# Layer 0, q and k: one 1x1 product per block of pixels for all 192 channels, into one z tile

## The chip, the cores and the metric

The kernel runs on one core of a Trainium2 chip. The metric is the device time of one execution in microseconds (us), as the median of several runs. Times inside an execution come from the hardware profile of one run. Its engines are PE (TensorE's matmuls), PEld (TensorE's weight loads, which overlap the matmuls), DVE (VectorE), ACT (ScalarE), POOL (GpSimd) and SP (SyncE, which here only issues transfers).

## What is computed

The input is an fp32 image batch of shape (4, 48, 256, 256). Four layers follow each other, and each adds to its input a function of the group-normalised input. The change lies in layer 0, which is, cut to what matters:

```python
hidden = conv1x1(gn(x), w_hidden) + b_hidden            # 48 -> 288 channels
qkv = depthwise3x3(hidden, w_dw) + b_dw                 # zero padding
q, k, v = split(qkv, 3)                                 # 96 channels each
out = irfft2(rfft2(q_patch) * rfft2(k_patch))           # on 8x8 patches
normed = (out - mean_c(out)) / sqrt(var_c(out) + eps)   # over the 96 channels
x = x + conv1x1(v * (normed * gamma + beta), w_out) + b_out
```

Layers 1 and 2 are gated layers with an 8x8 Fourier mask and a depthwise convolution; layer 3 gates 8x8 blocks by pooled values.

## The kernel before

Layer 0 works in two passes over the pixels. Each has N = 64 steps (4 images, 16 strips of 16 rows). The first pass makes q and k (192 channels), correlates their patches and keeps the normalised result in DRAM; the second makes v (96 channels), multiplies and projects. Both use the class `Strips`, once with `thirds` = 2 (name qk), once with `thirds` = 1 (name v). In the profile the tiles of the first carry `_qk`, those of the second `_v`.

A strip's 1x1 product, the method `mixed`, takes the pixels as the stationary operand. `xn` holds the strip as blocks of 6 rows by 18 columns, so that each block is 108 pixels with their borders. There are two halves of rows (u), sixteen blocks across (j) and two halves of the partitions (h, at partitions 0 and 64), 64 blocks in all. The stationary operand is one block, 49 input rows (48 channels and a row for the bias) by 108 pixels. The moving operand is the scaled weight matrix `w1`, restricted to 96 channels. The result, 108 pixels by 96 channels, goes into a PSUM tile `h_ps`, which holds four blocks j for both h, 768 values a partition. A copy on ACT or DVE, by turns, moves it to `z`, in the layout channel by block. There is one `z` tile for each third of 96 channels, `z0` and `z1`, each with a single buffer. For q and k a step is 128 products and 16 copies.

The method `depthwise` then multiplies, for each channel, the table `d` (109 pixels by 64 outputs) with that channel's 64 blocks of `z` (`c_ps`, L386). The pixels of `z` are rows 0 to 107; row 108 holds ones for the bias.

The loop of the first pass issues in step n: `mixed(n)`; `arrange(n+1)` on POOL, which fills `xn` from the loaded strip `x`; `load(n+2)`; `stats_ahead(n)`, which reads rows of the next image by transfers from ACT's queue into two `xstat` tiles and takes their statistics on DVE (L411); `attend(n-2)`; the transfers `fetch(n-1)` on SP; `convolve(n)`, the depthwise part with its copies `s` on ACT (L441) and their transfers on SP. `attend` is a chain: transform of q and k (`f_ps`, L478), copy of q on ACT (L490), product with k on DVE (L495), inverse transform (`o_ps`, L505), copy on ACT (L509); then the mean (`mu`, L520) on DVE, its subtraction on POOL (L522), the square on ACT (`sq`, L527), the variance on DVE (`var`, L529 and L530), the power and the scaling on POOL (L531, L532), the store (L533). The scaling of one half (`scale`) runs inside `convolve`.

All PSUM tiles of the pass share one pool of four buffers (`ps2`, 128 x 2 x 512). Each engine executes its own instructions in order. That order is made by a planner that starts from the order of the program, and puts an instruction where its own estimate of times lets it start; a few instructions in `attend`, marked `here`, keep the order of the program. The gated layers have an order of their own, pinned by hand.

Of the kernel before, what the change touches and what calls it, by code (L numbers as in the profile page):

```python
# [10 lines left out]
F32 = mybir.dt.float32  # L11
# [6 lines left out]
C = 48  # L18
# [155 lines left out]
def conv_stack_kernel(ctx: ExitStack, tc: tile.TileContext, t: dict):  # L174
    nc = tc.nc
# [44 lines left out]
    def evacuate(dst, src):  # L220
        turn[0] += 1
        if turn[0] % 2:
            nc.scalar.copy(dst, src)
        else:
            nc.vector.tensor_copy(dst, src)


    def layer0():
# [5 lines left out]
        NJ, PX, K = 16, 108, 109  # L234
# [17 lines left out]
        class Strips:  # L252


            def __init__(self, name, c_first, thirds, order, wp, sb, psum, spare, nx):
                self.name, self.c_first, self.thirds = name, c_first, thirds
                self.wp, self.sb, self.psum = wp, sb, psum
                nch = 96 * thirds
                self.d = d = wp.tile([K, nch, 64], F32, tag="d", name=f"d_{name}")
                for o in range(0, 64, 8):  # L260
                    basis = sb.tile([10, 8, K], F32, tag=spare[0], name=f"basis_{name}_{o}", bufs=spare[1])
                    nc.scalar.dma_start(basis, t["ones"][:, order, o : o + 8, :])
                    for i in range(0, 8, 2):
                        ps = self.ps2(f"d_ps_{name}_{o}_{i}")
                        for k in range(2):
                            nc.tensor.matmul(
                                ps[:K, k, :nch], basis[:, i + k, :],
                                taps[:, c_first : c_first + nch], start=True, stop=True,
                            )
                        evacuate(  # L270
                            d[:, :, o + i : o + i + 2],
                            ps[:K, :, :nch].rearrange("p n c -> p c n"),
                        )

                self.zs = [
                    wp.tile([K, 96, 64], F32, tag=f"z{m}", name=f"z_{name}_{m}") for m in range(thirds)
                ]
                for z in self.zs:
                    nc.gpsimd.memset(z[96:K], 1.0)


                self.xts = [
                    wp.tile([HC + 1, 10, W], F32, tag=f"x{i}", name=f"x_{name}_{i}") for i in range(nx)
                ]
                self.beside = [set() for _ in range(nx)]
                for xt in self.xts:
                    nc.gpsimd.memset(xt, 1.0)
                self.xn = wp.tile([HC + 1, 2, NJ, 6, 18], F32, tag="xn", name=f"xn_{name}")
                nc.gpsimd.memset(self.xn, 0.0)
# [63 lines left out]
            def mixed(self, n):  # L353
                b, s = steps[n]
                if s == 0:
                    self.weights_of(b)
                k = 0
                for m, z in enumerate(self.zs):
                    c0 = self.c_first + 96 * m
                    to = z[0:PX].rearrange("p c (h u j) -> p h c u j", h=2, u=2)  # L360
                    for u in range(2):
                        for j0 in range(0, NJ, 4):
                            ps = self.ps2(f"h_ps_{self.name}_{n}_{m}_{u}_{j0}")
                            for j in range(4):
                                for h in range(2):
                                    at = slice(64 * h, 64 * h + C + 1)
                                    nc.tensor.matmul(  # L367
                                        ps[0:PX, h, 96 * j : 96 * j + 96],
                                        self.xn[at, u, j0 + j].rearrange("p r c -> p (r c)"),
                                        self.w1[at, c0 : c0 + 96], start=True, stop=True,  # L370
                                    )
                            k += 1
                            copy = nc.scalar.copy if k % 2 else nc.vector.tensor_copy
                            copy(  # L374
                                to[:, :, :, u, j0 : j0 + 4],
                                ps[0:PX, :, 0:384].rearrange("p h (j c) -> p h c j", j=4),
                            )

            def depthwise(self, n, m, put):

                for q in range(3):
                    ps = self.ps2(f"c_ps_{self.name}_{n}_{m}_{q}")
                    for k in range(16):
                        for e in range(2):
                            c = 48 * e + 16 * q + k
                            nc.tensor.matmul(  # L386
                                ps[64 * e : 64 * e + 64, k // 8, 64 * (k % 8) : 64 * (k % 8) + 64],
                                self.d[:, 96 * m + c, :], self.zs[m][:, c, :], start=True, stop=True,
                            )
                    put(q, ps)  # L390


        with ExitStack() as st:
            wp = st.enter_context(tc.tile_pool(name="l0aw", bufs=1))
# [184 lines left out]
        with ExitStack() as st:  # L579
            wp = st.enter_context(tc.tile_pool(name="l0bw", bufs=1))  # L580
# [7 lines left out]
            for h in range(2):  # L588
                at, ch = slice(64 * h, 64 * h + C), slice(C * h, C * h + C)
# [113 lines left out]
            for b in range(B):  # L703
                ps = v.ps2(f"gn1_ps_{b}")
# [643 lines left out]
```

## Time and profile before

| what | value |
|---|---|
| time, median of 3 runs | 13026.5 us (13022.06 to 13051.78) |
| the profiled execution's own time | 13011.09 us |
| its span | 13009.1 us |
| mean granted TensorE clock | 0.945 |
| PE busy | 11869.5 us (91%) |
| PEld busy | 9389.8 us (72%) |
| DVE busy | 8029.6 us (62%) |
| ACT busy | 5848.6 us (45%) |
| POOL busy | 3678.6 us (28%) |
| first and last product of h for q and k | 152.4 and 3055.2 us |
| first and last product of h for v | 3207.0 and 5002.7 us |

The busy shares are means over four layers with different limits, so the first pass of layer 0 has to be read by itself, from 152 us to about 3085 us. A row of a group gives line, engine, operation, output and inputs, then for a matmul the stationary operand as rows times columns and the moving operand as rows by columns, then the number of instructions, their busy time and the mean time of one. After the second bar stands the idle time of the engine just before them and what ended it. Busy time counts overlapping instructions once. The duration of one matmul record is longer than its distance from the next, since they are pipelined: what it costs is read from the distance.

### The profile page before, as it was taken

Reading aid. Unit: us, or ns where it says so; the run is one execution under the profiler, and the core shown is the slowest. Engines: PE = TensorE matmul, PEld = TensorE weight load, DVE = VectorE, ACT = ScalarE, POOL = GpSimd, SP = SyncE. Lnnn points to the kernel's source line nnn. Section 1 sums busy time; section 2 is a strip of 40 time slices with the busy share of each in tenths; the row PEclk is TensorE's granted clock in tenths of the full one; section 3 lists DMA queues with packets and bytes.
Section 4 is the critical chain, followed back from the end, with each engine's and each line's share of the span. In section 5 each row is a group of like instructions: output and inputs, shape, how many; then the busy total and the mean of one; then the engine's idle time right before and its main releaser. Section 6 shows DMA issues by size and latency. Waiting matters only on the chain.

```text
span 13009.1 us, 473453 instructions
## 1 busy us (share of the span) xinstructions
PE 11869.5 (91%) x217556; PEld 9389.8 (72%) x217556; DVE 8029.6 (62%) x8422; ACT 5848.6 (45%) x7294; POOL 3678.6 (28%) x4549
## 2 busy tenths in 40 slices
PE   5899999998999999999998999989999989999976
PEld 5567777776888887777776777767777767777754
DVE  4666666665444444666665666665666666666678
ACT  1345555554444443444443444434444434444456
POOL 2356565665222222112112112111121121121111
PEclk8799999998999998999998999989999989999987
DMA  6666666664444443555554554544555545555555
GB/s 147 191 203 208 205 210 207 209 210 152 119 117 121 119 123 80 111 110 107 105 111 92 105 110 104 108 93 94 106 105 108 111 88 106 109 107 108 109 134 192
DMA packets 378785, 1708.61 MB, mean 131 GB/s; under 512 B 100181, under 2 KB 100786, under 8 KB 280802
## 3 DMA queue, kind: packets, MB, share of 16 engines
q1 hardware_dynamic: 202656, 907.70, 26.3%
q0 software_dynamic: 146560, 731.59, 24.1%
q10 hardware_dynamic: 27586, 39.03, 1.1%
q8 instruction: 1715, 28.10, 0.9%
q14 instruction: 268, 2.20, 0.1%
HBM read 832.42 MB, written 584.91 MB: 109 GB/s over the span
## 4 chain that ended last, share of the span: by engine, by line
PE 59%; DMA 13%; ACT 12%; DVE 8%; issue 5%; POOL 1%; SPq 1%; ACTq 0%; DVEq 0%; POOLq 0%
PE c_ps L955 14%; DMA z<-z 8%; PE y_ps L882 8%; ACT z L926 5%; ACT z L918 5%; PE h_ps_qk L367 4%; PE v_ps L647 4%; PE f_ps L478 3%; PE c_ps_qk L386 3%; PE h_ps_v L367 3%; PE c_ps_v L386 3%; PE xo_ps L992 3%; PE z_ps L908 3%; PE o_ps L505 2%; DMA xstat<-in_x 2%
## 5 line engine op out<-in xcount | busy, mean ns | idle before, releaser
L955 PEld LDWEIGHTS c_ps<-z,d 100*64 100x64 f32 x76032 | 2490.0, 146 | 788.5 <-issue 324.0
L955 PE MATMUL c_ps<-z,d 100*64 100x64 f32 x76032 | 2601.7, 230 | 416.9 <-DMA z<-z 161.4
L961 ACT ACTIVATE g<-c_ps 128x512 f32<-128x512 f32 x1188 | 695.7, 597 | 3544.7 <-PE c_ps L955 3539.7
L962 DVE TENSOR_TENSOR g<-g,c_ps 128x512 f32<-128x512 f32 x1188 | 802.6, 685 | 1599.8 <-ACT g L961 1599.6
L886 DVE TENSOR_TENSOR yf<-y_ps,mask 128x768 f32<-128x768 f32 x1536 | 1377.6, 951 | 413.5 <-PE y_ps L882 413.5
L882 PE MATMUL y_ps<-w_in,f 49*128 49x96 f32 x24576 | 1511.5, 279 | 21.6 <-issue 19.6
L882 PEld LDWEIGHTS y_ps<-w_in,f 49*128 49x128 f32 x24576 | 1445.0, 192 | 57.8 <-issue 22.3
L933 POOL DMA_DIRECT2D z<-z x384 | 200.3, 522 | 4515.6 <-ACT z L926 4426.3
L908 PE MATMUL z_ps<-yf,dft 64*64 64x512 f32 x9216 | 1104.8, 606 | 10.9 <-issue 4.5
L926 ACT COPY z<-z_ps 64x1024 f32<-64x1024 f32 x1024 | 1073.0, 1074 | 24.4 <-PE z_ps L908 5.6
L918 ACT COPY z<-z_ps 64x512 f32<-64x512 f32 x1536 | 856.6, 610 | 284.6 <-PE z_ps L908 251.1
L367 PE MATMUL h_ps_qk<-w_qk,xn_qk 49*108 49x96 f32 x16384 | 890.4, 270 | 60.5 <-DVE z_qk L374 48.2
L367 PEld LDWEIGHTS h_ps_qk<-w_qk,xn_qk 49*108 49x108 f32 x16384 | 864.7, 185 | 81.3 <-DVE z_qk L374 60.3
L966 DVE STREAM_TRANSPOSE g<-g 128x2048 f32<-128x2048 f32 x396 | 911.3, 2301 | 5.1
L992 PE MATMUL xo_ps<-g,w_out 24*64 24x512 f32 x12288 | 842.1, 599 | 28.7 <-ACT z L926 27.4
L926 DVE COPY z<-z_ps 64x1024 f32<-64x1024 f32 x512 | 619.4, 1210 | 399.7 <-DMA z<-carry 208.6
L386 PEld LDWEIGHTS c_ps_qk<-z_qk,d_qk 109*64 109x64 f32 x24576 | 777.8, 138 | 41.5 <-issue 29.5
L386 PE MATMUL c_ps_qk<-z_qk,d_qk 109*64 109x64 f32 x24576 | 788.3, 223 | 5.6 <-issue 5.4
L478 PE MATMUL f_ps<-t,l_fft 64*94 64x384 f32 x4096 | 758.1, 509 | 34.0 <-ACT f L490 31.6
L522 POOL TENSOR_TENSOR o<-o,mu 128x1536 f32<-128x1536 f32 x128 | 443.6, 3466 | 1109.4 <-DVE mu L521 813.9
L1000 DVE TENSOR_TENSOR res<-xo_ps,res 112x1024 f32<-112x1024 f32 x512 | 614.8, 1222 | 186.4 <-PE xo_ps L992 159.1
L992 PEld LDWEIGHTS xo_ps<-g,w_out 24*64 24x64 f32 x12288 | 298.7, 131 | 557.3 <-issue 221.4
(194 smaller groups left out, 17402.2 us busy)
## 6 DMA issues: line engine op xcount, KB each, us to landing
z<-z SPq DMA_DIRECT2D x1152, 203.9 KB
t<-s SPq DMA_DIRECT2D x512, 384.0 KB
t<-t SPq DMA_DIRECT2D x256, 768.0 KB
n<-o POOLq DMA_DIRECT2D x128, 768.0 KB, 5.2
kept<-n SPq DMA_DIRECT2D x128, 768.0 KB
xf<-x POOLq DMA_DIRECT2D x256, 384.0 KB, 11.7
res<-x POOLq DMA_DIRECT2D x248, 384.0 KB, 12.6
x<-res POOLq DMA_DIRECT2D x248, 384.0 KB, 5.4
```

The costliest lines, as they stand in the source:

```text
L367: nc.tensor.matmul(ps[0:PX, h, 96 * j : 96 * j + 96], self.xn[at, u, j0 + j].rearrange("p r c -> p (r c)"), self.w1[at, c0 : c0 + 96], sta ...
L386: nc.tensor.matmul(ps[64 * e : 64 * e + 64, k // 8, 64 * (k % 8) : 64 * (k % 8) + 64], self.d[:, 96 * m + c, :], self.zs[m][:, c, :], star ...
L478: nc.tensor.matmul(ps[0:94, e, 0:384], fft[at, 0:94], patches[n, m, r][at, rp, 24 * ch : 24 * ch + 24, :].rearrange("p c u -> p (c u)"), s ...
L882: first(i + j == 0, nc.tensor.matmul(ps[:, i, 96 * j : 96 * j + 96], f[at, 4 * h + j, :], w_in[at, m, :], start=True, stop=True,))
L886: pin(nc.vector.tensor_tensor(y[:, :, :, 4 * h : 4 * h + 4], ps[:, :, 0:384].rearrange("p i (j c) -> p c i j", j=4), mask[:, m].rearrange( ...
L908: first(q == 2 and p + v == 0, nc.tensor.matmul(to[64 * v : 64 * v + 64], dft[at, 1, at], y[at, c0 : c0 + 16].rearrange("p c i j -> p (c i ...
L918: pin(nc.scalar.copy(columns(p, 48 * v + 32, 48 * v + 48), last[64 * v : 64 * v + 64, p].rearrange("p (c i j) -> p c i j", i=2, j=16),))
L926: pin(copy(columns(p, 48 * v, 48 * v + 32), ps[64 * v : 64 * v + 64].rearrange("p q (c i j) -> p (q c) i j", i=2, j=16),))
L955: first(v + k == 0, nc.tensor.matmul(ps[p0 : p0 + 64, v, f0 : f0 + nj], d[rows, HID * v + 48 * m + c, :], z[rows, us, 48 * v + c, 1 : NP + ...
L962: pin(nc.vector.tensor_tensor(to, to, of[:, 1], ALU.mult))
L966: pin(nc.vector.transpose(flat, flat))
L992: first(i + k == 0, nc.tensor.matmul(ps[h][k // 2][64 * i : 64 * i + 64, k % 2, :], w_out[at, m, :], gs[m][at, j0 : j0 + 16].rearrange("p ...
```

## The change

`mixed` multiplies a block of pixels once by all the channels of the pass (`nch` = 96 x `thirds`, so 192 for q and k) where it multiplied it once for each third. A PSUM tile then holds `per` = 384 / `nch` blocks j, two for q and k, with the channels of a block side by side; it still holds 768 values a partition. The loop over thirds is gone, so a step of q and k issues 64 products in place of 128, and 16 copies as before, by turns on ACT and DVE, beginning with ACT. `z` becomes one tile of `nch` channels. A copy writes 192 channels with runs of two neighbouring blocks, where it wrote 96 channels with runs of four. `depthwise` reads channel 96 m + c of this tile. For v, `nch` is 96 and `per` is 4, and the products, the copies and the turns are as before.

```diff
-                self.zs = [
-                    wp.tile([K, 96, 64], F32, tag=f"z{m}", name=f"z_{name}_{m}") for m in range(thirds)
-                ]
-                for z in self.zs:
-                    nc.gpsimd.memset(z[96:K], 1.0)
+                self.z = wp.tile([K, nch, 64], F32, tag="z", name=f"z_{name}")
+                nc.gpsimd.memset(self.z[96:K], 1.0)
...
-                k = 0
-                for m, z in enumerate(self.zs):
-                    c0 = self.c_first + 96 * m
-                    to = z[0:PX].rearrange("p c (h u j) -> p h c u j", h=2, u=2)
-                    for u in range(2):
-                        for j0 in range(0, NJ, 4):
-                            ps = self.ps2(f"h_ps_{self.name}_{n}_{m}_{u}_{j0}")
-                            for j in range(4):
-                                for h in range(2):
-                                    at = slice(64 * h, 64 * h + C + 1)
-                                    nc.tensor.matmul(
-                                        ps[0:PX, h, 96 * j : 96 * j + 96],
-                                        self.xn[at, u, j0 + j].rearrange("p r c -> p (r c)"),
-                                        self.w1[at, c0 : c0 + 96], start=True, stop=True,
-                                    )
-                            k += 1
-                            copy = nc.scalar.copy if k % 2 else nc.vector.tensor_copy
-                            copy(
-                                to[:, :, :, u, j0 : j0 + 4],
-                                ps[0:PX, :, 0:384].rearrange("p h (j c) -> p h c j", j=4),
-                            )
+                nch = 96 * self.thirds
+                per = 384 // nch
+                to = self.z[0:PX].rearrange("p c (h u j) -> p h c u j", h=2, u=2)
+                for u in range(2):
+                    for j0 in range(0, NJ, per):
+                        ps = self.ps2(f"h_ps_{self.name}_{n}_{u}_{j0}")
+                        for j in range(per):
+                            for h in range(2):
+                                at = slice(64 * h, 64 * h + C + 1)
+                                nc.tensor.matmul(
+                                    ps[0:PX, h, nch * j : nch * j + nch],
+                                    self.xn[at, u, j0 + j].rearrange("p r c -> p (r c)"),
+                                    self.w1[at, self.c_first : self.c_first + nch],
+                                    start=True, stop=True,
+                                )
+                        copy = nc.scalar.copy if (j0 // per) % 2 == 0 else nc.vector.tensor_copy
+                        copy(
+                            to[:, :, :, u, j0 : j0 + per],
+                            ps[0:PX, :, 0:384].rearrange("p h (j c) -> p h c j", j=per),
+                        )
...
-                                self.d[:, 96 * m + c, :], self.zs[m][:, c, :], start=True, stop=True,
+                                self.d[:, 96 * m + c, :], self.z[:, 96 * m + c, :], start=True, stop=True,
```

## The prediction

> **What bounds the kernel now.** I began with the long stretches. The table of stretches gives busy time of PE (matmuls), PEld (weight loads), DVE, ACT and POOL, each followed by its number of instructions, then the granted clock and the DMA share.
>
> ```profile
> 150.00:800.00 650.00, 543.16 (x7523) 412.33 (x7525) 381.76 (x422) 232.78 (x272) 227.82 (x156) 0.80 0.63 190
> 800.00:1500.00 700.00, 678.55 (x12213) 528.24 (x12213) 474.74 (x400) 396.83 (x459) 429.52 (x268) 1.00 0.63 208
> 1500.00:2200.00 700.00, 678.93 (x12020) 527.65 (x12018) 471.86 (x403) 393.91 (x458) 432.08 (x275) 1.00 0.63 209
> ```
>
> The touched stage, q and k of layer 0, runs from 152 to 3085 us, in 64 steps. It has two regimes. From 800 us PE is busy 97% of the time at full clock. Before that the clock is 0.80 and PE often idles. The starts of the 64 groups of 256 h matmul records say the same: steps 0 and 1 take 38 and 37 us, steps 2 to 9 about 70 (the last 57), and nearly all later ones 42.5. The groups of the stage by shape, over the whole run, give the durations:
>
> ```profile
> L367 PE MATMUL h_ps_qk<-w_qk,xn_qk 49*108 49x96 f32 x16384 | 890.4, 270 | 60.5 <-DVE z_qk L374 48.2 <-ACT s L441 8.3 <-ACT w_qk L351 3.0
> L478 PE MATMUL f_ps<-t,l_fft 64*94 64x384 f32 x4096 | 758.1, 509 | 34.0 <-ACT f L490 31.6 <-ACT o L509 2.4
> L374 DVE COPY z_qk<-h_ps_qk 108x768 f32<-108x768 f32 x512 | 483.5, 952 | 187.2 <-PE h_ps_qk L367 187.2
> L374 ACT COPY z_qk<-h_ps_qk 108x768 f32<-108x768 f32 x512 | 409.5, 800 | 457.2 <-PE h_ps_qk L367 353.5 <-DVE z_qk L374 85.5 <-DVE stats L411 8.5
> ```
>
> A step writes 128 products at L367 and the record count is 256 per step: each fp32 product is two passes. The reader should see that PE's main wait before h is for DVE's copy of z. The chain of waits shows when, in a late step (start, length, piece):
>
> ```profile
> 1536.91 1.02 ACT s L441
> 1537.92 1.40 ACT sq L527
> ...
> 1539.34 2.85 DVE var L529
> ...
> 1542.21 1.78 DVE var L530
> 1543.99 0.87 DVE z_qk L374
> ...
> 1544.90 8.62 PE h_ps_qk L367 x176
> ```
>
> So the end is not set by PE alone. h starts at 1540.54 and fills five PSUM tiles (80 passes); four buffers exist. Tile 2 belongs to DVE, which is still at var until 1543.99, so PE stands for 0.33 us; then come 11 tiles (176 passes) on the chain. In the trace that gap after pass 80 stands in nearly every late step.
>
> **What the Trainium skill says.** "TensorE: Matmul & The Clock Gate", section "LDWEIGHTS (loading the stationary operand)", prices a load by its columns over 1.2 GHz; 108 columns give 90 ns (estimate). The trace agrees: two passes on the two row groups (h=0 and h=64) go as a pair, and pairs follow each other every 95 ns at full clock. The same page, "Step-by-step: what each phase is for", says the next weights are pulled ahead of a running matmul. Here the load starts about 12 ns after the previous matmul starts, so a pair costs the longer of load and stream. Which one it is, f shows: 384 columns, 24 passes in 3.87 us, 322 ns a pair, or 0.84 ns a column, with 94-column loads hidden. 96 columns would stream in 80 ns; so h is now bound by its loads. "VectorE: DVE Perf Modes", section "Why PSUM operands drop a tier", leaves fp32 copies out of PSUM no faster mode, whatever their pattern; the trace's z copies stay at 0.96 us.
>
> **The change, part by part.**
> - Products: 64 a step with 192 columns in place of 128 with 96. Their weight loads halve, the columns streamed stay. A pair is now 95 ns; after, 192 x 0.84 = 161 ns, taken as 162, above the 95 of the load. A PSUM tile goes from 8 pairs, 0.76 us, to 4 pairs, 0.65 us. Sixteen tiles: 12.16 to 10.4 us, so PE has 1.76 us less to do in a step. Bounds for the pair, which this trace does not show: 160 (pure stream) and 190 (twice today's, nothing gained). I take 162 because f shows the stream rule with loads of nearly the same width.
> - What of it counts: DVE's var does not move, since it hangs on the step's earlier o, not on h. Five tiles will be ready at 1540.54 + 3.25 = 1543.79 in place of 1544.34, and PE still waits until 1544.90: the wait grows from 0.33 to 0.88 us, and 0.55 us of the 1.76 is lost there. On the path are 11 tiles x 0.11 = 1.2 us.
> - Next in line are the copies. Two tiles take PE 1.30 us; ACT needs 0.80, DVE 0.96 of that. They are hidden, with 0.34 us of air on DVE. Where other DVE work uses up this air, as the statistics do in steps 0 to 9, every further us of it holds PE for a us.
> - Copies: still 16 a step of 768 elements, ACT and DVE in turn. Runs of z fall from four elements to two. The d tables are written by just such runs of two, with these durations:
>
> ```profile
> L223 ACT COPY d_qk<-d_ps_qk x16: 480/481/490, 8.6 to 50.5; 109x384 f32<-109x384 f32 x16
> L225 DVE COPY d_qk<-d_ps_qk x16: 557/558/559, 9.8 to 51.7; 109x384 f32<-109x384 f32 x16
> ```
>
>   From these to 768 elements DVE adds 0.40 us for 384 elements, or 1.04 ns each, ACT 0.32 us. Runs of two cost nothing: zero, bounds -0.05 and +0.05 us a copy.
> - One z tile: a copy of step n+1 now touches channels of both thirds and waits for all 192 depthwise channels, where the first eight waited for the first third. But PE takes h after c anyway (c ends at 1540.6), so nothing new is late. The first c now needs all 16 copies. In the late steps f and o, 21 us, stand between; in steps 0 and 1 nothing does, and each may lose one copy, 1.2 us with its hand-over: 2.4 us. The ones in z are set by one memset in place of two of 5.2 us, long before 152 us: zero.
> - xn: its first half is last read after half of h, earlier three quarters. POOL's arrange (L324) and the load behind it (L312) have some 30 us until the next h: zero.
> - v has one third; its products, copies and order stay. No DMA is added, removed or moved past another on SP or POOL.
>
> Sum: steps 10 to 63 are 54. Fifty with the wait give 50 x 1.2 = 60, four near image starts without it (16, 17, 32, 48) 4 x 1.76 = 7. Steps 0 to 9 are set by the statistics: 192 bn_stats at L411 run as far ahead as they can, 22 or so a step, one every 3.1 us, DVE behind the DMA of xstat and ACT's queue behind DVE. There h spans 25 us for 12 us of work. A faster h gains between 0 and 3.5 us a step (at half clock); I take 1, together 10. Less the 2.4: 75 us. The profiled run had a span of 13009.1 and a time of 13011.1 us, 15.4 below the median of 13026.5 of the runs; 75 us off the latter is **12951 us**.
>
> **Rivals.**
> - *The wait at tile 6 goes.* The order on each engine is a planner's, by its own times. If DVE takes its first z copies ahead of var, a step gains 1.76 + 0.33 = 2.1 us, 54 x 2.1 = 113, with the early steps some 125: 12,900. For it: h now gives tile 2 earlier. Against: var is older work and was put first in nearly all steps.
> - *Nothing from the products.* If a pair of 192 columns takes twice today's 95 ns, 190, the loads not being what holds h, the time stays at 13,026. Against it stands f's 0.84 ns a column.
> - *Slower: the copies run in turn.* One tile, both engines writing all channels in runs of two interleaved by columns: if the planner takes neighbouring copies as overlapping, each waits for the one before. Two tiles then take 0.80 + 0.96 + about 0.1 = 1.86 us, against 1.52 now. From 1543.99 fifteen copies last 13.9 us, to 1557.9, where the last now ends at 1554.5: up to 3.4 us a step late, at the least half of it, so 92 to 184 us over 54 steps, 13,118 to 13,210. It decides once two copies with their hand-overs exceed 1.52 us, in most pairs. Against it: before, columns were interleaved in the same way, by fours, and ACT's third tile (1543.10) was copied before DVE's second (1543.90).
> - *The order of the statistics.* A step among the first ten costs 27 us more than a late one. If the planner spreads the same 192 over one step more or less, that is about 27 us either way; it widens every case and makes none alone.
>
> **How the numbers follow.** The likely case 0.60, its own range 12,920 to 12,990; the wait gone 0.12; nothing 0.12; slower 0.16. 0.3% is 39 us, about what a measurement of this kernel can tell from no change. Faster by more: 0.12 and 0.58 of the first, 0.70. Within: 0.12 and 0.02, 0.14. Slower: 0.16. The range from 12,885 to 13,040 takes in the first three and leaves out the slower one.
>
> **What would show it.** L367 with 8192 records of 49x192, pairs 162 ns apart, 0.65 us a tile; the gap after the fifth tile 0.9 us; late steps of 41.3 us; z copies at 0.80 and 0.96 us; ACT's third before DVE's second; about 22 statistics in a step until step 10. I am wrong if pairs come near 190 ns, if z copies wait for z copies, or if late steps stay at 42.5 us.

## The result, and the profile after

The changed kernel took 12941.3 us against 13036.2 for the kernel before on the same chip; the ratio is 0.9932, with a 95% interval of 0.9907 to 0.9956. Run once more with more rounds it took 12931.9 against 13011.1, ratio 0.9945 (0.9934 to 0.9957). The forecast of 75 us less was a ratio of 0.9942.

The lines that answer to those of before, from the groups by shape of the first profiled run after the change:

```profile
L363 PE MATMUL h_ps_qk<-w_qk,xn_qk 49*108 49x192 f32 x8192 | 740.2, 336 | 80.5 <-DVE z_qk L370 70.9 <-ACT s L437 4.5 <-ACT w_qk L348 3.0
L474 PE MATMUL f_ps<-t,l_fft 64*94 64x384 f32 x4096 | 759.1, 508 | 39.2 <-ACT f L486 31.9 <-DVE z_qk L370 4.8 <-ACT o L505 1.9
L370 DVE COPY z_qk<-h_ps_qk 108x768 f32<-108x768 f32 x512 | 483.9, 953 | 107.8 <-PE h_ps_qk L363 100.7
L370 ACT COPY z_qk<-h_ps_qk 108x768 f32<-108x768 f32 x512 | 424.8, 830 | 354.4 <-PE h_ps_qk L363 237.4 <-DVE z_qk L370 100.6 <-DVE stats L407 7.0
```

There are half as many records, each of 192 columns, with 740 us of busy PE in place of 890. PE's wait for DVE's z copies rose from 48 to 71 us, and DVE's wait for PE fell from 187 to 101: part of the work taken from PE came back as a wait. The chain of waits in a late step (one of the steps 10 to 63) shows where (start, length, piece):

```profile
1552.76 1.01 ACT s L437
1553.78 1.40 ACT sq L523
1555.19 2.82 DVE var L525
1558.04 1.71 DVE var L526
1559.75 0.87 DVE z_qk L370
1560.66 7.40 PE h_ps_qk L363 x88
```

The same pieces stand in the same order; only the last is shorter, 7.4 us where it was 8.6. The instructions of PE for the five tiles before the wait, and for the 88 passes behind it, which are called the tail here:

```profile
1556.39 3.50 PE L363 MATMUL h_ps_qk<-w_qk,xn_qk 49*108 49x192 f32 x40
1560.66 7.40 PE L363 MATMUL h_ps_qk<-w_qk,xn_qk 49*108 49x192 f32 x88 [0.77 <-DVE z_qk L370]
```

From start to start, a pair of passes follows the one before it every 163 ns, the median of the late steps in both runs of this kernel; it was 95 ns before. The stretches of the stage (busy PE, PEld, DVE, ACT, POOL, then clock, DMA share, GB/s):

```profile
150.00:800.00 650.00, 512.84 (x6500) 356.46 (x6500) 389.94 (x428) 244.70 (x280) 235.96 (x160) 0.85 0.64 193
800.00:1500.00 700.00, 668.56 (x10026) 505.71 (x10027) 485.70 (x415) 407.09 (x470) 439.07 (x278) 1.00 0.65 215
```

PE is a little less busy in the late steps, 95.5% for 97%, although these steps are shorter.

The q and k stage, from its first h to its last c, took 2932.7 us before, 2858.2 in the first profiled run after and 2849.6 in the second: 75 and 83 us less. The first of these two runs was only 32.5 us shorter over its span, since its v and gated stages took 23 and 29 us more, and the rest 10 us less. From the first product of v onward DVE, ACT and POOL execute the same instructions in the same order as before, and in the second run v took 1839.9 us (1834.0 before) and the gated layers 7355.8 (7339.7). Over the ten profiles of this document v ranges from 1832.5 to 1862.8 us, so runs of these stages differ by tens of us without any change to them. Yet the three kernels with products of 96 columns for q and k have the three shortest v stages (up to 1838.3 us, where the other seven begin at 1838.4). A small loss outside the touched stage is therefore not excluded, and its cause would be open. The runs below are compared by the q and k stage as well.

### The profile page after: what moved, and what is told of

Read it like the earlier page. It is cut to its first block, busy times and chain, and to the rows that moved or that the text cites. A ratio compares the mean times of both kernels' runs of the same rounds, so it can differ in the third digit from the quotient of the medians.

```text
span 12976.6 us, 457080 instructions
## 1 busy us (share of the span) xinstructions
PE 11763.0 (91%) x209364; PEld 9242.1 (71%) x209364; DVE 8033.2 (62%) x8422; ACT 5868.2 (45%) x7294; POOL 3684.4 (28%) x4548
## 4 chain that ended last, share of the span: by engine, by line
PE 59%; DMA 13%; ACT 12%; DVE 8%; issue 5%; POOL 1%; SPq 1%; ACTq 0%; DVEq 0%; POOLq 0%
PE c_ps L951 14%; PE y_ps L878 9%; DMA z<-z 8%; ACT z L922 5%; ACT z L914 4%; PE v_ps L643 4%; PE c_ps_qk L382 4%; PE f_ps L474 3%; PE h_ps_qk L363 3%; PE h_ps_v L363 3%; PE c_ps_v L382 3%; PE xo_ps L988 3%; PE z_ps L904 3%; PE o_ps L501 3%; DMA xstat<-in_x 2%
## 5 line engine op out<-in xcount | busy, mean ns | idle before, releaser
L363 PE MATMUL h_ps_qk<-w_qk,xn_qk 49*108 49x192 f32 x8192 | 740.2, 336 | 80.5 <-DVE z_qk L370 70.9
L363 PEld LDWEIGHTS h_ps_qk<-w_qk,xn_qk 49*108 49x108 f32 x8192 | 685.6, 176 | 121.0 <-DVE z_qk L370 94.8
```

Source lines behind the costliest of these rows:

```text
L363: nc.tensor.matmul(ps[0:PX, h, nch * j : nch * j + nch], self.xn[at, u, j0 + j].rearrange("p r c -> p (r c)"), self.w1[at, self.c_first : ...
```

## The experiments

### The changed kernel again

> The changed kernel once more, with more rounds. By the theory (64 wide products, the wait for DVE before the sixth PSUM tile grown to 0.9 us) late steps of 41.3 us and a q and k stage some 75 us shorter than before, so 75 us less in all (ratio 0.994); v and the gated layers have the same order of instructions and differ by noise alone. If the first profile's longer v and gated stages (+23 and +29 us) belong to the change, they are there again, and the gain is near 35 us.

Measured: ratio 0.9945, median late step 41.35 us (42.54 before), the q and k stage 83 us shorter. The first ten steps took 597.0 us (617.4 before, 605.2 in the first run after), the other 54 took 2252.6 (2315.3 before, 2253.0).

### One z tile alone

```diff
-                self.zs = [
-                    wp.tile([K, 96, 64], F32, tag=f"z{m}", name=f"z_{name}_{m}") for m in range(thirds)
-                ]
+                self.z = wp.tile([K, nch, 64], F32, tag="z", name=f"z_{name}")
...
-                    to = z[0:PX].rearrange("p c (h u j) -> p h c u j", h=2, u=2)
+                    to = self.z[0:PX, 96 * m : 96 * m + 96].rearrange("p c (h u j) -> p h c u j", h=2, u=2)
```

> Before, with one z tile of 192 channels in place of two of 96, products and copies unchanged (96 columns, runs of four). Theory: no cost and no gain, within 10 us of before, late steps 42.5 us. If the single tile makes the copies run in turn or wait, late steps of 44 us and over, 92 to 184 us slower. If the gain of the change came from the tile, 75 us faster.

Measured: ratio 1.000 (0.9989 to 1.0012), late steps 42.55 us, the stage 2938.5 us (2932.7 before). The single tile neither costs nor gains, and late steps of 44 us and over, which copies in turn would have given, are not there.

### Two products of 96 in the new layout

```diff
-                            for h in range(2):
-                                at = slice(64 * h, 64 * h + C + 1)
-                                nc.tensor.matmul(
-                                    ps[0:PX, h, nch * j : nch * j + nch],
+                            for m in range(self.thirds):
+                                c0 = self.c_first + 96 * m
+                                for h in range(2):
+                                    at = slice(64 * h, 64 * h + C + 1)
+                                    nc.tensor.matmul(
+                                        ps[0:PX, h, nch * j + 96 * m : nch * j + 96 * m + 96],
...
```

> After, but each block of pixels is multiplied by two sets of 96 columns, one after the other, into the same PSUM tile: 128 products a step again, the copies, the single z tile and runs of two kept. Theory (loads of 108 columns bound a 96-column pair at 95 ns): PSUM tiles 0.76 us apart, late steps 42.5 us, the time of before within 20 us. If layout, copies or the single tile made the gain, late steps of 41.3 us and 75 us faster than before.

Its group of h, and the piece of h in the chain of a late step:

```profile
L365 PE MATMUL h_ps_qk<-w_qk,xn_qk 49*108 49x96 f32 x16384 | 887.6, 270 | 52.9 <-DVE z_qk L372 48.2 <-ACT w_qk L348 3.0 <-ACT s L439 1.2
```

```profile
1553.72 8.63 PE h_ps_qk L365 x176
```

Measured: ratio 1.0002 (0.9989 to 1.0014), late steps 42.56 us, the stage 2941.3 us. With the layout, the tile and the copies of the change, but 128 products a step, everything of before is back: the busy time, the wait and the 8.6 us of the tail. The gain is that of the halved products alone.

### The first four copies on ACT

```diff
-                        copy = nc.scalar.copy if (j0 // per) % 2 == 0 else nc.vector.tensor_copy
+                        k = (NJ // per) * u + j0 // per
+                        act = k % 2 == 0 if self.thirds == 1 else k < 4 or k % 2
+                        copy = nc.scalar.copy if act else nc.vector.tensor_copy
```

> After, with the copies of the first four PSUM tiles of a step of q and k all on ACT, then DVE and ACT in turn (10 on ACT, 6 on DVE). Theory: the wait before the sixth tile goes, since ACT is free from 1.1 us after the start of h while DVE is at var until 3.45; late steps fall from 41.3 to 40.2 us, 54 x 1.1 = 60 us less than after, 135 us less than before. If the chain of o, mu, sq and var sets the step whatever h does, the wait only moves to f or o, and late steps stay at 41.3 us.

ACT's and DVE's instructions in a late step of this kernel, then its chain (start, length):

```profile
1551.93 2.99 ACT L372 COPY z_qk<-h_ps_qk 108x768 f32<-108x768 f32 x4
```

```profile
1552.57 1.82 DVE L528 TENSOR_SCALAR var<-var 128x16 f32<-128x16 f32 x1
1554.47 0.96 DVE L372 COPY z_qk<-h_ps_qk 108x768 f32<-108x768 f32 x1
```

```profile
1540.14 10.85 PE c_ps_qk L384 x368
1550.99 10.58 PE h_ps_qk L363 x128
1561.57 3.87 PE f_ps L476 x24
```

ACT clears four tiles while DVE is at var. The 128 passes of h now stand in one piece right after c, with no wait between, and var has left the chain. The edit also takes two of DVE's eight copies from it; that this is not what counts is seen in the tail, whose pairs stay 163 ns apart: what went is the wait, 1.03 us of the 1.1 us that a step lost. Measured: late steps 40.23 us, the stage 2782.5 us, 67 less than in the second run after (51.6 in the 54 late steps, 15.6 in the first ten); ratio to before 0.9895 (0.9874 to 0.9916), 12868.9 us. The wait did not move on to f or o.

### Three xstat tiles

This kernel and those below ran on another chip, on which the kernel before took 13014.3 us (13011.1 on the first). The ratios are to the runs on the same chip, the stages are compared across the two.

```diff
-            xstat = [wp.tile([HC, 2, W], F32, tag=f"xstat{i}", name=f"xstat{i}") for i in range(2)]
+            xstat = [wp.tile([HC, 2, W], F32, tag=f"xstat{i}", name=f"xstat{i}") for i in range(3)]
```

> After, with three xstat tiles in place of two. Theory: the first ten steps (some 600 us, against 413 for ten late ones) are paced by the round trip of a statistic's load, 3.1 us for each of 192 with two tiles in flight; with three some 2.1 us, 400 us for all of them, so 50 to 150 us faster than after, late steps unchanged at 41.3. If the steps are slow for another reason (the half clock of PE by itself, the first fetches), the first ten stay at 600 us.

Measured: ratio 0.9895 (0.9866 to 0.9924). The late steps stay at 41.36 us, the first ten take 545.5 us, the stage 2795.9, 54 less than in the second run after: the lower end of what was expected. A statistic came every 2.5 us (3.06 with two tiles), not every 2.1, and the planner put 25 into a step in place of 21. So the two tiles set a part of that pace; what sets the rest was not tried.

### No statistics of images 1 to 3

```diff
                 if b + 1 < B:
-                    for r0 in range(10 * s, min(10 * s + 10, 128), 2):
-                        xstat.append(xstat.pop(0))
-                        stats_of(b + 1, r0, xstat[-1], 2)
+                    in_coefs[b + 1] = in_coefs[0]
```

> After, without the statistics of images 1 to 3 (192 loads pairs and bn_stats left out; these images are scaled with the mean and deviation of image 0). Theory: the first ten steps run like late ones, 41 us from step 2 on, so the q and k stage is shorter by some 180 us. If they stay at 65 us, the statistics are not what sets them.

The kernel leaves these statistics out, and scales images 1 to 3 with those of image 0. It was executed once. The first stretch of its table of stretches:

```profile
150.00:800.00 650.00, 610.39 (x9597) 475.99 (x9598) 421.84 (x363) 368.99 (x425) 377.70 (x250) 0.99 0.63 210
```

Measured: steps 0 and 1 took 27.9 and 27.3 us, the next 40.2 to 42.5; the stage took 2643.0 us, 207 less than in the second run after, where some 180 were expected. The granted clock of this stretch is 0.99, where it was 0.85 and 0.86 in the two runs after. In those runs 29% of the pairs of h in the first ten steps lie some 320 ns apart, twice the 163; here 2% do. The half clock came with PE's waits and went with them.

### The loads of xstat on SP

```diff
-                    queue = nc.scalar if rows == 2 else nc.sync
+                    queue = nc.sync
```

> After, with the loads of xstat issued on SP's queue in place of ACT's. Theory: ACT's copies no longer stand behind loads that wait for a free xstat, so h, f and o of the first ten steps go on while a load is out, 50 to 150 us faster than after. Against it: on SP the loads stand behind the transfers t, which wait for the s copies, and the fetches of t stand behind loads; then the first steps stay at 65 us or get slower.

Measured: ratio 0.9938 (0.9916 to 0.9959), as for the change alone. The first ten steps fell to 439.8 us, and yet the stage took 2832.5, only 17 us less: the planner now put six statistics into each of the next steps, to about step 31, and such a step takes some 48 us in place of 41.4. Six of them cost 6.7 us, 1.1 us each. Left out altogether they had been worth 207 us / 192 = 1.1 us each. Neither side of this expectation came true: the first steps did get fast, but nearly all the time came back later.

### Both

> After, with the first four copies of a step on ACT and three xstat tiles. Theory: the two gains lie in different steps and add: late steps 40.2 us and a shorter start, 110 to 210 us less than after. If ACT's added copies hold up its loads of xstat, the start gains less than with three tiles alone.

Measured: ratio 0.984 (0.9807 to 0.9873), 12832.2 us, the fastest of the kernels here that leave nothing out. Late steps 40.23 us, the first ten 533.5, the stage 2731.4, 118 us less than in the second run after; the two alone gave 67 and 54. The gains add, within 3 us.

## Why the prediction was right or wrong

- **Products: right.** A pair of 192 columns takes 163 ns (162 forecast, bounds 160 and 190). With 96 columns in the same layout the tail was 8.63 us again. So h had been held by its weight loads, as the Trainium skill's price for 108 columns said (page "TensorE: Matmul & The Clock Gate", section "LDWEIGHTS (loading the stationary operand)"): 90 ns by that estimate, 95 in the trace. A fixed cost of every product would explain the experiments as well, but the gated layers of the kernel before speak against it. They stream the same 96 columns with weights of 128 columns:

```profile
L882 PE MATMUL y_ps<-w_in,f 49*128 49x96 f32 x24576 | 1511.5, 279 | 21.6 <-issue 19.6 <-ACT z L926 0.9 <-ACT w_in L798 0.7
```

  Their pairs follow each other every 112 ns (median), 17 ns more than those of h for 20 more columns of weights, and the pairs of c, with weights of 64 columns, every 58 ns. After the change h is held by its stream: 0.85 ns a column, f has 0.84.
- **What of it counts: right.** In the median late step the start after pass 40 follows the one before it by 1.19 us, 1.03 more than without a wait; before, it was 0.58 us after pass 80, 0.49 more. The wait grew by 0.54 us (0.55 forecast; in the step shown by less, from 0.33 to 0.77 us), and late steps fell by 1.2 us to 41.35. The four copies on ACT show the cause: without that wait a late step takes 40.23 us, the 1.1 us that DVE's var held back.
- **Copies: small miss.** DVE kept its 0.96 us, but ACT's copy went from 799 to 832 ns, within the bound of 0.05 and hidden. The kernel with two products of 96 has the 833 ns as well, so it belongs to the layout, not to the wide product. The d tables, from which the prediction took no cost, did not show it.
- **One z tile: right in the sum, low in the part.** Alone it changed nothing, and with it alone c has no wait for copies that the profile shows. The predicted wait of c for the last copies in steps 0 and 1 comes with the new layout, in which every copy writes channels of both thirds (it is there, with 3.5 us, with two products of 96 too). It took 5.3 us in two waits of the second run where 2.4 was put down; without the statistics it takes 2.3:

```profile
PE c_ps_qk L382 <- DVE z_qk L370: 5.3, 2, 2.7
L382 PE MATMUL c_ps_qk<-z_qk,d_qk 109*64 109x64 f32 x24576 | 786.1, 223 | 8.5 <-issue 5.9 <-DVE z_qk L370 2.3
```

  The first line is of the second run after, the other of the kernel without statistics. So the forecast was right for the copies and left out that DVE has statistics to do in these steps.
- **The first ten steps: right about what sets them, low in size.** Without statistics they run like late ones. They gained 12 and 20 us in the two runs, against 10 less 2.4. The planner put 21 statistics into a step for 22, at the same 3.1 us each. The 1 us a step was a guess between 0 and 3.5, and by which wait the faster h gains here was not tried; the kernels with products of 96 differ by up to 9 us in these steps.
- **The sum.** Late steps gave 62 us (67 forecast), early ones 12 to 20 (8): 75 and 83 us in the stage for 75 forecast. That the first run hit the 75 exactly is luck: one part was 5 us too high, the other 4 too low. The medians of the whole kernel moved by 95 and 79 us, with the noise of the later stages in them.
- **The rivals.** Copies in turn: refuted; in a late step ACT's second copy began at 1558.64, ahead of DVE's first, at 1559.66, which stands before it in the program. Nothing from the products: refuted by the 163 ns. The wait gone: it did not happen by itself, since var kept its place on DVE, but made by hand it brought what that rival promised: 150 us less in the stage than before, where 125 was reckoned: 114 in the late steps (113 reckoned) and 36 in the first ten (12). The order of the statistics: nine of them moved into step 9, which went from 56.8 to 65 us, but the last of the 192 was in that step as before, so no slow step came or went.

## What to carry to other kernels

Look at a matmul's distance from the next and ask whether it matches the columns of the stationary or those of the moving operand; where the loads set it, one wider product on the same weights can cost less than two narrow ones: here 163 ns a pair, set by the stream, where two pairs took 190. Before adding up what PE saves, find the copy that frees its next PSUM buffer: the tiles made before that copy gain nothing. Then give those first copies to the engine that is idle at that moment; here that gave 67 us, nearly as much as the 75 to 83 of the change itself.

## What was not expected of the hardware

ACT's copy out of PSUM of 768 values took 799 ns with runs of four values in the output and 832 ns with runs of two; DVE's took 957 and 958. The 192 statistics cost about 1.1 us each, 20 to a step in ten steps or six to a step in thirty with their loads on SP, though a bn_stats lasts only 0.69 us: spreading them did not hide them. Why the price is the same in both places was not tried.
